# Spare row buffers joined, the four-head attention ended block by block, loads and readback moved in a four-layer graph network

## The chip, the cores and the metric

The kernel runs on one core of a Trainium2 chip. The number that counts is device time in microseconds (us), smaller is better; a profile shows one further execution of the same program, with every instruction on each engine: PE (TensorE matmuls; PEld its weight loads), DVE (VectorE), ACT (ScalarE), POOL (GpSimd) and SP (which only issues transfers). A name with a q, such as SPq or ACTq, is an engine's queue of issued work.

## What is computed

Four layers run over a graph of 2708 nodes with 256 features each. Every layer adds a graph attention over the neighbours and then a feed-forward part, both on layer-normed features. The change touches layer 1 (four attention heads, then a top-1 mixture of eight experts) and the beginnings of the attentions of layers 2 and 3. Cut to these:

```python
def L1_gnn(x, adj, W, a1, a2):                   # 4 heads of 64
    h = (x @ W).reshape(n, 4, 64)
    si = einsum('nhd,d->nh', h, a1); sj = einsum('nhd,d->nh', h, a2)
    e = leaky_relu(si[:, None, :] + sj[None, :, :], negative_slope=0.2)
    att = softmax(where(adj[:, :, None] > 0, e, -9e15), axis=1)
    return einsum('ijh,jhd->ihd', att, h).reshape(n, 256)

def L1_ffn(x, W1, b1, Wg, bg, Wd, bd):           # 8 experts
    H = gelu(x @ W1 + b1, approximate=False)     # 1024 wide
    probs = softmax(H @ Wg + bg)
    assign = argmax(probs)
    for e in range(8):
        out = out + where((assign == e)[:, None], probs[:, e:e+1] * (H @ Wd[e] + bd[e]), 0)
    return out

x = x + L1_gnn(layernorm(x), adj, ...)
x = x + L1_ffn(layernorm(x), ...)
x = x + L2_gnn(layernorm(x), adj, ...)           # one head, with a bias
x = x + L2_ffn(layernorm(x), ...)                # attention and a top-2 mixture
x = x + L3_gnn(layernorm(x), adj, ...)           # one head, then elu
x = x + L3_ffn(layernorm(x), ...)                # linear
```

## The kernel before

The nodes are 22 tiles of 128 rows (the last has 20), and most loops go by six blocks of 512 columns, that is four tiles each and two in the last. The residual X stays in the on-chip buffer for the whole program. The order of instructions on each engine is made by a scheduler from the program; `issue_after` holds one instruction behind another, and each engine takes its own list in that order.

`gat_heads` (L678) takes two heads in each of two passes p. For each source tile j it makes the masked weights e for the two heads on ACT (L674) and DVE (L675), and PE adds up the six accumulators of values (L780) and the denominators (L788) over all j. After the last j of a pass the denominators are copied (ds, L798), transposed, and inverted (rd, L803 and L806). Then each block's accumulator is copied out (o, L810), transposed (aux, L815), multiplied by the inverse (y, L822) and added to X (L829). Both passes end this way, and only then does `top1_ffn` begin.

`top1_ffn` (L857) has a front part by blocks. It loads the gate weights wg, biases and w1 on POOL's queue (L871 to L892) and the experts' weights wd, 8 MB, on SP's. The layer norm's sums and roots of all blocks are taken by `ln_stats`. For each block: `features` norms and transposes four tiles into ft, `hidden` makes 1024 hidden values per node (h, L911, then Gelu L915), `gate` makes the logits (pq L937, pr L943) and the routing bookkeeping, and `store` transposes the hidden values into rows (L926), copies them by DVE and ACT in turn into one of three buffers hr (L927), and writes them to a table in memory (`hidden`, L930, on SP's queue). The stores of the last two blocks come together at the end. The bookkeeping also scatters each node's number into a table by expert slot (fnodes, L1444).

Then come 26 expert steps of 128 slots each. The node numbers are read back from the table: the first eight steps by one load (L1554), whose every element of 4 bytes goes to its own partition, the others by one load each (L1550). They are cast to integers (L980) in groups of up to four steps, and POOL gathers the hidden rows by them (L990), five buffers deep and four steps ahead. Each step transposes its rows (ht, L1003, copied by DVE or ACT at L1004), multiplies by the expert's weights (y, L1035, two accumulators), adds the expert's bias bd (ys, L1041) and sends the rows to a table of results (L1573, POOL). During step 3 a `Head` (L1066) folds the score vectors of the next attention into its weight: loads g2w (L1074), av (L86) and g2bv (L1082), eight DVE operations at L657 and L660, and the bias's part (L1084 to L1089). Its loads and bd are issued on ACT's queue.

`gat_single` (L1092) is the attention of layers 2 and 3. It begins with `combine` (L1583): all results are read back (y, L1594), by SP's and ACT's queues in turn, and each block is weighted and added to X on DVE (L1604), followed by its statistics (L144, L145), the root on ACT (sd, L147), rstd (L151) and the normed tiles (L108) that PE transposes (tp, L1134). In layer 3 the mask of neighbours is also read back (`reload_graph`, L2088); `mark_empty` (L2080) writes two pieces of flags into it through ACT's queue. The same `mark_empty` runs before the four-head attention.

## Time and profile before

| | us |
|---|---|
| median of 3 runs (2875.14 to 2881.12) | 2879.4 |
| the profiled execution | 2876.56 |
| its span | 2874.8 |
| PE busy | 2630.7 |
| DVE busy | 1448.3 |
| ACT busy | 1037.4 |
| POOL busy | 369.4 |
| mean granted clock of PE, share of full speed | 0.951 |

The span is the time from the first to the last instruction of the profiled execution; 1.8 us lie around it. An engine's busy time leaves out the issuing of transfers and waiting on semaphores. The stages that the change touches lie at these places of the span: the four-head attention from 690 to 1068 us, the front part of the top-1 mixture from 1068 to 1209, the store and routing between 1209 and 1245, its expert steps from 1245 to 1360, the start of layer 2's attention from 1360 to 1374, and that of layer 3's from 2553 to 2578.

### The profile page before, as it was taken

The numbers are of one execution on the slowest core, as the hardware profiler recorded it, in microseconds if no ns is written. First come the engines' busy times: TensorE is split into PE (matmuls) and PEld (weight loads), VectorE is DVE, ScalarE is ACT, GpSimd is POOL, SyncE is SP. The second block draws the span as 40 slices with busy tenths as digits, with TensorE's granted clock in tenths as the row PEclk, the third lists the DMA queues.
The fourth block names the chain that finished last, engine by engine and source line by source line (L and its number), as shares of the span: only waits on it lengthen the run. The fifth ranks groups of instructions, "written<-read, shape, count | busy, mean of one in ns | idle before, by whom it ended". The sixth has DMA issues, their size and how long they took to land. (4 is left out here: it accounts for less than half of the span.)

```text
span 2874.8 us, 32363 instructions
## 1 busy us (share of the span) xinstructions
PE 2630.7 (92%) x11709; PEld 1604.0 (56%) x11709; DVE 1448.3 (50%) x3078; ACT 1037.4 (36%) x1636; POOL 369.4 (13%) x456
## 2 busy tenths in 40 slices
PE   5999989799999998979899899999969999969998
PEld 4667746563333334568688533333337777747885
DVE  7753358354777774432644456455653222235455
ACT  3344433224665653311543223233322222225453
POOL 0000012100000001133200023223331111110002
PEclk9999999698999998989999999899979999989999
DMA  8899210000000005253300100002031010041001
GB/s 296 290 301 327 81 65 1 8 1 1 1 1 1 1 17 176 82 173 108 114 1 0 34 22 17 15 0 93 15 116 32 30 34 30 30 147 49 1 1 39
DMA packets 113727, 197.67 MB, mean 69 GB/s; under 512 B 12380, under 2 KB 71636, under 8 KB 110732
## 3 DMA queue, kind: packets, MB, share of 16 engines
q1 hardware_dynamic: 92758, 147.89, 15.8%
q0 software_dynamic: 13120, 38.06, 4.1%
q10 hardware_dynamic: 7690, 9.62, 1.1%
q8 instruction: 98, 1.61, 0.2%
q14 instruction: 61, 0.50, 0.1%
HBM read 135.82 MB, written 59.71 MB: 68 GB/s over the span
## 5 line engine op out<-in xcount | busy, mean ns | idle before, releaser
L675 DVE SCALAR_TENSOR_TENSOR e<-e,mask 128x768 f32<-128x768 f32 (+2 forms) x264 | 411.5, 1573 | 311.0 <-ACT e L674 310.8
L674 ACT ACTIVATE e<-big_p,minus_one,ratio 128x768 f32<-128x768 f32 (+2 forms) x264 | 394.9, 1513 | 363.4 <-PE acc L1236 230.0
L1236 PE MATMUL acc<-V,e 128*128 128x257 f32 (+1 forms) x1936 | 433.5, 383 | 4.5 <-DVE e L675 4.4
L1236 PEld LDWEIGHTS acc<-V,e 128*128 128x128 f32 (+1 forms) x1936 | 352.4, 186 | 85.6 <-issue 32.1
L780 PE MATMUL acc<-e,V 128*64 128x512 f32 (+1 forms) x1056 | 249.7, 550 | 4.1 <-DVE e L675 4.1
L1909 PE MATMUL h<-w,ft 128*128 (+1 forms) x752 | 233.6, 453 | 0.5 <-ACT ft L1891 0.5
L284 PE MATMUL acc<-F,e 128*128 128x257 f32 x968 | 226.3, 384 | 2.9 <-DVE e L281 2.5
L284 PEld LDWEIGHTS acc<-F,e 128*128 128x128 f32 x968 | 173.5, 185 | 66.8 <-DVE e L281 28.1
L780 PEld LDWEIGHTS acc<-e,V 128*64 128x64 f32 x1056 | 95.4, 137 | 180.7 <-issue 159.1
L1736 PE MATMUL sc<-qt,kt 64*128 64x512 f32 (+5 forms) x568 | 176.6, 574 | 4.1 <-ACT e L1749 2.4
L1749 ACT ACTIVATE e<-sc 128x1024 f32<-128x1024 f32 (+3 forms) x120 | 99.6, 859 | 190.9 <-PE sc L1736 174.4
L1909 PEld LDWEIGHTS h<-w,ft 128*128 128x128 f32 x752 | 136.2, 191 | 56.7 <-issue 1.4
L281 DVE TENSOR_TENSOR e<-e,mask 128x512 f32<-128x512 f32 (+2 forms) x132 | 80.5, 625 | 150.4 <-ACT e L275 148.7
L1761 DVE TENSOR_TENSOR sum<-sum,e 128x1024 f32<-128x1024 f32 (+4 forms) x88 | 99.8, 1135 | 79.3 <-ACT e L1749 76.4
L275 ACT ACTIVATE e<-score 128x512 f32<-128x512 f32 (+2 forms) x132 | 69.7, 544 | 178.9 <-PE score L273 152.2
L1941 PE MATMUL po<-w,ht 114*128 (+1 forms) x564 | 129.5, 379 | 0.9 <-DVE ht L1934 0.9
L1755 PE MATMUL po<-e,V 128*64 128x512 f32 (+3 forms) x480 | 112.2, 549 | 16.8 <-ACT e L1749 8.7
L788 PE MATMUL den<-e,low 128*3 128x512 f32 (+1 forms) x1056 | 123.1, 542 | 0.0
L1941 PEld LDWEIGHTS po<-w,ht 114*128 114x128 f32 x564 | 106.7, 189 | 22.6 <-DVE ht L1934 8.2
L1563 DVE TENSOR_SCALAR second<-f,down 128x1 f32<-128x1 f32 x47 | 9.9, 212 | 213.0 <-DMA f<-hs 213.0
L273 PE MATMUL score<-QK 128*128 128x512 f32 (+2 forms) x264 | 112.1, 555 | 1.2 <-ACT e L275 0.7
L1736 PEld LDWEIGHTS sc<-qt,kt 64*128 64x128 f32 (+1 forms) x568 | 60.4, 189 | 92.5 <-issue 76.4
(606 smaller groups left out, 3496.3 us busy)
## 6 DMA issues: line engine op xcount, KB each, us to landing
row<-in_adj SPq DMA_DIRECT2D x21, 1354.0 KB
raw<-in_adjT SPq DMA_DIRECT2D x35, 768.0 KB
hs<-zero SPq DMA_DIRECT2D x8, 2838.0 KB
hidden<-hr SPq DMA_DIRECT2D x42, 256.0 KB
wd<-in_f_wd SPq DMA_DIRECT2D x8, 1024.0 KB
kept<-mask SPq DMA_DIRECT2D x21, 338.5 KB
mask<-kept SPq DMA_DIRECT2D x21, 338.5 KB
f<-hs SPq DMA_DIRECT2D x47, 129.0 KB
```

The costliest lines, as they stand in the source:

```text
L273: nc.tensor.matmul(ps[:r, :iw], QK[:, 0, span(j)], QK[:, 1, i0 : i0 + iw], start=True, stop=True)
L284: nc.tensor.matmul(acc[k][:ri], e[:r, k * P : k * P + ri], F[:r, j, :], start=j == 0, stop=j == NT - 1)
L674: nc.scalar.activation(v, big_p[:, i], AF.Relu, bias=net.minus_one, scale=ratio)
L675: return nc.vector.scalar_tensor_tensor(v, v, 1.0, net.mask[:, j, i], ALU.add, ALU.mult)
L780: nc.tensor.matmul(acc[n][half, :iw], V[:, j, h, :], e[:, k, i0 : i0 + iw], start=j == 0, stop=j == NT - 1)
L788: nc.tensor.matmul(den[g : g + Q, :iw], low[:, j, h, Q - 1 - q : 2 * Q - 1 - q], e[:, k, i0 : i0 + iw], start=False, stop=j == NT - 1 and ...
L1236: nc.tensor.matmul(acc[k][:ri], e[:, k * P : k * P + ri], V[:, j, :], start=j == 0, stop=j == NT - 1)
L1736: nc.tensor.matmul(by_pairs(ps[:r, g])[:, :, o:], kt[b, span(j)], qt[b, :, o:iw], start=True, stop=True)
L1755: nc.tensor.matmul(by_pairs(po[b])[:, :, o:], V[:r, j, g, :], by_pairs(e[:r, g])[:, :, o:], start=j == 0, stop=j == last,)
L1761: (nc.gpsimd if part else nc.vector).tensor_tensor(total, total, ev, ALU.add)
L1909: last = nc.tensor.matmul(halves[s, n][:, q, :HALF], fts[s][:, c, :], weights.w13[n][:, es[s], c, q * HALF : (q + 1) * HALF], start=c == 0 ...
L1941: last = nc.tensor.matmul(po, ht[:KP, k, :], w2[:KP, es[s], k, :], start=k == 0, stop=k == KC - 1)
```

## The change

- `gat_heads` is called inside `top1_ffn`. The copies o of all six blocks and the inverses rd are kept in a pool of their own. Pass 0 adds its blocks as before; pass 1 returns a function that adds one block. In the last step j of each pass the denominators come before the values; elsewhere after.
- `top1_ffn` adds block 0, takes its sums, adds block 1, and makes features of block 0; blocks 1 and 2 follow, then the hidden values of block 0; blocks 3 to 5 are added after that. `turn` chains these steps. The roots of blocks 1 to 5 are made on DVE by Newton steps (`newton`, some ten small operations per call), not on ACT.
- The experts' weights wd are placed where the kept copies were, and loaded two experts at a time after the stores of blocks 0 to 3.
- The stores of blocks 4 and 5 are all copied by ACT; the first eight of the twelve go through spare buffers: two of ft, cut in two, and one of the hidden halves, cut in four.
- The node numbers are read as rows of 128 (the first read as eight contiguous pieces of 512 bytes), transposed on PE and cast from there, in groups of eight and nine.
- bd is loaded on POOL's queue after the fourth gather; the head's three loads go to POOL's queue, after the send of step 3.
- In `gat_single` the zeroing of V and ratio goes from POOL to DVE, and a small root (`warm`) is asked of ACT at the start.
- `combine` reads by SP and POOL in turn, and by ACT only the second choice of block 0. The mask's reload is issued after the last read on POOL; the flags are written through POOL's queue.

```diff
-def gat_heads(net):
+def gat_heads(net, keep):
+    o = keep.tile([P, len(cols), 4 * P], F32, name="o")
+    rds = [keep.tile([P, 4, 4, Q], F32, name=f"rd{p}") for p in range(2)]
+    def add(p, n, psum, tag):
+        i0, iw = cols[n]
+        its = tiles_of(i0, iw)
+        pt = psum.tile([P, 4, P], F32, name="aux", tag=tag)
+        for c, i in enumerate(its):
+            r = rows(i)
+            nc.tensor.transpose(pt[:r, c, :], o[:, n, c * P : c * P + r], net.ident)
+        y = o[:, n, :].rearrange("p (c k d) -> p c k d", c=4, k=2)
+        for c0, c1, r in whole_and_rest(its):
+            d = rds[p].rearrange("p c (k b) q -> p c k b q", b=2)[:r, c0:c1, :, n // Q, n % Q]
+            nc.vector.tensor_tensor(
+                y[:r, c0:c1],
+                pt[:r, c0:c1, :].rearrange("p c (k d) -> p c k d", d=DH),
+                d.unsqueeze(3).to_broadcast([r, c1 - c0, 2, DH]),
+                ALU.mult,
+            )
+            xs = X[:r, its[0] + c0 : its[0] + c1, p * 2 * DH : (p + 1) * 2 * DH]
+            last = nc.vector.tensor_tensor(xs, xs, y[:r, c0:c1].rearrange("p c k d -> p c (k d)"), ALU.add)
+        return last
...
+            def values(e, j):
...
+            def weights(e, j):
...
+            for j in range(NT):
+                e = wide.tile([P, 2, N], F32, name="e")
+                for k, h in enumerate(heads):
+                    gat_pairs(net, e[:, k, :], j, 0, N, big_p[:, h, :], ratio[:, j, h : h + 1])
+                for step in (values, weights) if j + 1 < NT else (weights, values):
+                    with tc.issue_after(last.ins):
+                        last = step(e, j)
...
+                if p == 0:
+                    add(p, n, paux, "aux")
+    return lambda n, psum, tag: add(1, n, psum, tag)
...
+        held = ExitStack()
+        add = gat_heads(net, held.enter_context(tc.tile_pool(name="g1keep", bufs=1, side="right")))
-        wd = inner.enter_context(tc.tile_pool(name="f1wd", bufs=1, side="right")).tile([P, E, KC, D], F32, name="wd")
-        for e in range(E):
-            nc.sync.dma_start(wd[:, e], a["f1_wd"][e].rearrange("(c p) m -> p c m", p=P))
...
+            last = None
+            def turn(step, *args, **kw):
+                nonlocal last
+                with tc.issue_after(last.ins) if last else nullcontext():
+                    last = step(*args, **kw)
...
-            def store(its, halves):
+            def store(its, halves, late=False, room=()):
+                room = list(room)
                 for k, t in enumerate(its):
                     r = rows(t)
                     for n, half in enumerate(halves):
-                        hr = rp.tile([P, 512], F32, name="hr", bufs=3)
+                        hr = room.pop(0) if room else rp.tile([P, 512], F32, name="hr", bufs=3)
                         ps = pg.tile([P, 4, P], F32, name=f"hr{n}")
                         for c in range(KC // 2):
                             nc.tensor.transpose(ps[:r, c, :], half[:, c, k * P : k * P + r], net.ident)
-                        (nc.scalar.copy if n else nc.vector.tensor_copy)(
+                        (nc.scalar.copy if n or late else nc.vector.tensor_copy)(
                             hr[:r], ps[:r].rearrange("p c m -> p (c m)")
                         )
-                        nc.sync.dma_start(rows_of[span(t), n * 512 : (n + 1) * 512], hr[:r])
+                        last = nc.sync.dma_start(rows_of[span(t), n * 512 : (n + 1) * 512], hr[:r])
+                return last
...
+            tiles = [(tiles_of(*b)[0], tiles_of(*b)[-1] + 1) for b in blocks]
+            turn(add, 0, ptp, "tp")
+            turn(stats.sums, *tiles[0])
+            turn(add, 1, ptp, "tp")
+            turn(stats.roots, *tiles[0])
             ft = features(tiles_of(*blocks[0]))
+            turn(stats.sums, *tiles[1], root=False)
+            turn(add, 2, ptp, "tp")
+            turn(stats.sums, *tiles[2], root=False)
+            turn(stats.newton, rp, tiles[1][0], tiles[2][1])
             for n, (n0, nw) in enumerate(blocks):
                 its = tiles_of(n0, nw)
                 halves = hidden(ft, nw)
                 if n + 1 < len(blocks):
                     ft = features(tiles_of(*blocks[n + 1]))
+                if n == 0:
+                    for m in range(3, len(blocks)):
+                        turn(add, m, ptp, "tp")
+                        turn(stats.sums, *tiles[m], root=False)
+                    turn(stats.newton, rp, tiles[3][0], NT)
+                    last = None
+                    held.close()
+                    wd = inner.enter_context(tc.tile_pool(name="f1wd", bufs=1, side="right"))
+                    wd = wd.tile([P, E, KC, D], F32, name="wd")
                 gate(its, halves, nw)
                 kept.append((its, halves))
-                if n + 2 != len(blocks):
-                    for k in kept:
-                        store(*k)
-                    kept.clear()
+                if n + 2 < len(blocks):
+                    stored = store(*kept.pop())
+                    with tc.issue_after(stored.ins):
+                        for e in range(2 * n, 2 * n + 2):
+                            nc.sync.dma_start(wd[:, e], a["f1_wd"][e].rearrange("(c p) m -> p c m", p=P))
+            spare = [work.tile([P, 2, 512], F32, name="spare", tag="ft") for _ in range(2)]
+            spare.append(work.tile([P, KC // 2, 512], F32, name="spare", tag="ht512", bufs=3))
+            room = [t[:, k, :] for t in spare for k in range(t.shape[1])]
+            for k in kept:
+                store(*k, True, room)
+                room = ()
...
-            nc.scalar.dma_start(bd.rearrange("p e d -> p (e d)"), a["f1_bd"].rearrange("e d -> (e d)").partition_broadcast(P))
...
+            groups = [range(E)] + [range(s, min(s + 9, usual)) for s in range(E, usual, 9)]
+            rowed = sp.tile([P, P], F32, name="rowed", bufs=1)
             held = {}
-            def numbers(group):
+            def load(group, at):
+                node = rowed[at : at + len(group), :]
+                if group[0] == 0:
+                    route.load_first(node)
+                else:
+                    for k, s in enumerate(group):
+                        route.load(s, node[k : k + 1, :])
+            def numbers(group, at):
                 g = slice(group[0], group[-1] + 1)
-                nc.vector.tensor_copy(number[:, g], node[:, g])
-            def places(group):
+                here = slice(at, at + len(group))
+                ps = pt.tile([P, len(group)], F32, name="node", bufs=1)
+                nc.tensor.transpose(ps, rowed[here, :], net.ident[here, here])
+                nc.vector.tensor_copy(number[:, g], ps)
+                return ps
...
+            for n, g in enumerate(groups):
+                load(g, 32 * n)
+            first = numbers(groups[0], 0)
             for s in range(4):
-                fetch(s)
+                fetched = fetch(s)
+            with tc.issue_after(fetched.ins):
+                nc.gpsimd.dma_start(
+                    bd.rearrange("p e d -> p (e d)"), a["f1_bd"].rearrange("e d -> (e d)").partition_broadcast(P)
+                )
...
-                    route.send(to[:, s : s + 1], y)
-                    with tc.issue_after(added.ins):
-                        for g in groups[1:]:
+                    sent = route.send(to[:, s : s + 1], y)
+                    with tc.issue_after(added.ins), tc.issue_after(sent.ins):
+                        for n, g in enumerate(groups):
                             if s + 6 == g[0]:
-                                numbers(g)
-                                places(g)
+                                places(g, numbers(g, 32 * n))
                         if s == 3:
-                            heads.append(Head(net, prep, one, "g2", True, nc.scalar))
+                            heads.append(Head(net, prep, one, "g2", True))
...
-        nc.gpsimd.memset(V[:, LAST], 0.0)
-        nc.gpsimd.memset(ratio[:, LAST:], 0.0)
+        nc.vector.memset(V[:, LAST], 0.0)
+        nc.vector.memset(ratio[:, LAST:], 0.0)
+        nc.scalar.activation(small.tile([P, 1], F32, name="warm", bufs=1), net.ln_eps, AF.Sqrt)
...
-        self.loaded = sync.dma_start(f, self.hs[bass.ds(row, P), :])
+        rows_of = self.hs[bass.ds(row, P), :]
+        self.loaded = sync.dma_start(f, rows_of.rearrange("p d -> d p") if self.choices == 1 else rows_of)
     def load_first(self, f):
         self.loaded = self.net.nc.sync.dma_start(
-            f, self.hs.rearrange("(e c) d -> c (e d)", e=self.E)[:P, :]
+            f, self.hs.rearrange("(e c) d -> e (c d)", e=self.E)[:, :P]
...
+        queues = nc.sync, nc.gpsimd
...
-                    (nc.sync, nc.scalar)[(n + c) % 2].dma_start(
+                    engine = nc.scalar if n == 0 and c else queues[(n + c) % 2]
+                    read = engine.dma_start(
                         y[:r, k0:k1, :],
                         self.ys[r0 : r0 + (k1 - k0 - 1) * P + r, :].rearrange("(t p) d -> p t d", p=r),
                     )
+                    if engine is nc.gpsimd:
+                        self.read = read
...
-        reload_graph(net, kept)
+        with net.tc.issue_after(route.read.ins):
+            reload_graph(net, kept)
...
-        gat_heads(net)
...
-    net.nc.scalar.dma_start(row[:, :whole], net.flags[:LAST])
-    net.nc.scalar.dma_start(row[:, whole:], net.flags[LAST:NT, : N - whole])
+    net.nc.gpsimd.dma_start(row[:, :whole], net.flags[:LAST])
+    net.nc.gpsimd.dma_start(row[:, whole:], net.flags[LAST:NT, : N - whole])
```

The order of the pools in `gat_heads` also changes; `Stats` (L126) and `inverse_root` (L307) are as before.

## The prediction

> **What bounds the kernel now.** I read the engine totals first, then the forty slices and the chain of waits, then windows and timelines of the places that the edits touch.
>
> ```profile
> PE 2630.7 (92%) x11709; PEld 1604.0 (56%) x11709; DVE 1448.3 (50%) x3078; ACT 1037.4 (36%) x1636; POOL 369.4 (13%) x456
> ```
>
> TensorE works in 92% of the 2874.8 us span, so 244 us are idle, and they lie in the seams between stages. The chain of waits is followed back only to about 2146 us, so the earlier seams had to be read by windows. The columns below are window, length, busy time (and instructions) of PE, PEld, DVE, ACT, POOL, granted clock, DMA share, GB/s.
>
> ```profile
> 1068.23:1093.36 25.13, 9.50 (x37) 5.44 (x36) 23.34 (x92) 3.65 (x8) 4.63 (x13) 0.56 0.60 185
> 1093.36:1110.16 16.80, 16.80 (x36) 7.47 (x37) 2.41 (x7) 6.09 (x8) 0.00 (x0) 0.85 0.92 293
> 1110.16:1131.50 21.34, 21.31 (x96) 11.26 (x95) 7.21 (x28) 7.73 (x12) 4.00 (x4) 1.00 0.27 100
> ```
>
> Seam A is the first line: from the last denominator matmul of the four-head attention to the first hidden matmul (h, L911). VectorE is the busy one, 23.3 of 25.1 us: it adds all six blocks and takes their statistics before block 0 may go. Lines two and three are hidden(0) and the rest of the first block; there PE is full and DVE has room.
>
> Seam B is the end of that front part. Timeline columns: start, length, engine, line, operation, and in brackets the idle time before it and its releaser.
>
> ```profile
> 1223.27 0.58 ACT L927 COPY hr<-hr 128x512 f32<-128x512 f32 x1 [7.29 <-DMA hidden<-hr]
> 1226.53 0.68 DVE L927 COPY hr<-hr 20x512 f32<-20x512 f32 x1 [0.69 <-DMA hidden<-hr]
> 1231.44 0.41 SPq L1554 DMA_DIRECT2D node<-fnodes  x1
> 1238.78 0.17 DVE L980 CAST number<-node 128x8 int32<-128x8 f32 x1 [6.26 <-DMA node<-fnodes]
> 1239.84 1.00 POOL L990 DMA_INDIRECT hr<-hidden,number  x1 [22.18 <-DMA node<-fnodes]
> 1245.11 1.30 PE L1003 MATMUL ht<-ident,hr 128*128 128x128 f32 x5 [17.14 <-issue]
> ```
>
> Row copies wait for stores to free three buffers; the table read starts when all stores are in, takes 7.3 us to the cast, and the gather another 5.3 us. In the expert steps after it nothing waits long, and the fold of the next layer's scores runs at once:
>
> ```profile
> 1265.55 0.42 DVE L1041 TENSOR_TENSOR ys<-y,bd 128x256 f32<-128x256 f32 x1 [2.73 <-PE y L1035]
> 1265.89 0.41 DVE L657 TENSOR_TENSOR a1t<-g2w,av 128x256 f32<-128x256 f32 x1
> 1270.79 0.68 DVE L1004 COPY ht<-ht 128x512 f32<-128x512 f32 x1
> ```
>
> Seam D, from the decoder's experts to the last attention:
>
> ```profile
> 2557.22 12.66 ACTq L1594 DMA_DIRECT2D y<-dys  x7
> 2562.37 3.26 DVE L1604 SCALAR_TENSOR_TENSOR X<-y,dweight,X 128x256 f32<-128x256 f32 x8 [6.58 <-DMA y<-dys]
> 2575.12 1.28 ACT L147 ACT_TABLE_LOAD   x1 [22.31 <-DMA y<-dys]
> 2576.74 0.18 DVE L151 RECIPROCAL rstd<-sd 128x4 f32<-128x4 f32 x1 [6.23 <-ACT sd L147]
> 2577.52 1.73 PE L1134 MATMUL tp<-ident,f 128*128 128x128 f32 x7 [25.12 <-DVE f L108]
> ```
>
> The statistics of block 0 were ready at 2567.4, yet ACT takes the root only at 2576.4, because its queue is still issuing and waiting for loads.
>
> **Seam A, block-by-block end: -10.** The last step's matmuls are the same, in another order; the denominator's copy (0.69) and transposes now pass under the values. I count from the end of the last matmul, 1068.23. Removed ahead of h: the adds and statistics of blocks 3 to 5, and waits between. What stays in DVE's order: the copy of add (1.09), the copy of o (0.99 with its tail), rd and reciprocal (0.65), two blocks of y and X (4 x 0.69 = 2.7), block 0's statistics (1.9), then for four tiles normed (0.38), PE transposes, copy (0.39), with the waits seen now in the last two tiles, about 4. That sums to 11.3; I take 11.5. The loads of w1 are issued where they were, 3.8 us after the last matmul, and landed 5.2 later, at 9.0: just covered; if they took hyout's 12.7 us instead, h would start at 16.5. So h moves from 25.1 to 11.5: -13.6. Given back: the last three blocks' ten transposes (1.11 + 1.08 + 0.69 us at half clock, some 1.6 warm) now stand in a full PE. DVE's work for these blocks, 3.2 + 3.2 + 1.9, and ten small operations of the inverse root (2), is 10.3 us; added to 7.2 busy of 21.3 in that block it is 17.5, so throughput covers it. But DVE obeys order: the gate's copies and the row copies stand behind, PE waits for them, and ten of those 10 us are the upper price. I take 2. Net -10, bounds -13.6 and -2.
>
> **Block loads of the expert weights: 0.** Eight megabytes leave the stretch 1081 to 1112 and go in four parts behind the stores of blocks 0 to 3 on SP. Each part of 2 MB at the 348 GB/s of that stretch is 6 us; a block lasts 21, and the next stores come in its second half. Without that cover the row copies would wait up to 6 us per block, against ACT and DVE that are a third busy.
>
> **Spare row buffers: -6.** Twelve copies at 0.58 on ACT alone, with transposes, need about 9 us from 1209.7, where now the last is at 1228.5. The transfers cannot be drained so fast: the DMA share from 1210 to 1229 (0.71, 0.75, 0.86, 0.49 over 4 us each, 0.31 over 3) makes 12.2 us of full engines, so the end of all stores lies between 1222 and the present 1231. The twelfth copy also still waits for the ninth store. I take 1225.4, -6; bounds -9 and 0.
>
> **Table order: -3.4.** The first read has 8 descriptors rather than 1024 elements. Small loads landed in 2.1 to 3.0 us, the gathers in 5.2; I take 3.0. To it come a transpose (0.43, cold) and two hand-overs, 0.9 together. 7.3 - 3.0 - 0.9 = 3.4; bounds -4.3 and -1.2. Transposes and casts of the later groups cost PE under 1 us, in steps of 4.33 us.
>
> **Later bias loads: +3.4.** The bias bd is asked for after the fourth gather and first needed 7.5 us after PE starts; w1, as large and on the same queue, landed in 5.2, so it is covered. The head's three loads are worse. They go to POOL behind the send of step 3, which issued at 1266.25 (0.99); g2w follows at 1267.55. The g3 head did exactly this:
>
> ```profile
> 2149.07 0.79 POOL L1074 DMA_DIRECT2D g3w<-in_g_w  x1 [0.30 <-issue]
> 2155.04 0.43 DVE L657 TENSOR_TENSOR a1t<-g3w,av 128x256 f32<-128x256 f32 x1 [2.84 <-DMA av<-in_g_a]
> ```
>
> 5.9 us from issue to first use, so the fold starts at 1273.5, where now it starts at 1265.89. It waits in DVE's queue with ys of step 4 and the copy ht of step 6 behind it. Eight fold operations 0.33 apart (2.7), bt 0.6, ys 0.33, grow 0.6, ht 0.69 end at 1278.4; PE needs ht of step 6 at about 1275 (ys of step 5 was at 1274.21, plus transposes). The stall is 3.4; bounds 0 (loads in 2.1) and 6.
>
> The Trainium skill prices it lower: "DMA: Bandwidth & Descriptors", in its anatomy of a GpSimd-issued transfer, fits about 2.0 us plus bytes over 436e3 per us, 2.6 us for 256 KB. By that the fold would start near 1271 and the stall be about 1 us, the total 2.4 lower. The rows (3.8 and 5.1 us to landing) differ from it.
>
> **Readback, seam C: 0.** X waits for the first load on SP, which stays. The second block's load goes from ACT to POOL; it may land 1 us later, but DVE reaches it 3.3 us after the first. The root's table load (1365.77) was already over before it was needed, so asking for it early changes nothing here. The memsets of V and ratio (0.31, 0.10) pass from POOL to DVE, which idles until 1368.21. Bounds -1 and +1.
>
> **Readback, seam D: -5.** ACT keeps one load, so the root follows the statistics at 2567.4. Next late is DVE itself: the combination of block 1 stands ahead of rstd and ends at 2570.5; rstd and normed bring PE to 2571.3 rather than 2577.5, -6.2. Three queues at once instead of two may delay block 0's pair: a third 0.5 MB at 349 GB/s is 1.5 us. I take -5; bounds -6.2 and 0. The mask reload starts about as before and is needed 35 us later.
>
> A rule speaks against this: the same page ("SWDGE vs HWDGE vs iDMA") wants plain transfers on SP or ACT, not GpSimd. By it alone the term would be 0 or a loss; the row shows ACT's issuing as the thing waited for, so I keep the gain.
>
> **Start of the attention: -0.6.** The two flag loads (0.88, 0.75) leave ACT ahead of the first e; part of that was waiting on PE anyway. Bounds -1 and 0.
>
> **Sum.** -10 + 0 - 6 - 3.4 + 3.4 + 0 - 5 - 0.6 = -21.6. The profiled execution took 2876.6, so 2855.0. The median of the runs stood 2.8 above that execution; I add half and forecast 2856. A 0.2% difference, 5.8 us, is about what can be told from no change.
>
> **Rivals.** (1) The stores of seam B end when they do now, because the transfers and not the buffers are the limit: for it, a DMA share of 0.86 at only 65 GB/s around 1220; against it, the drop to 0.31 at the end. Time 2862. (2) The pushed-back DVE work of seam A lies wholly on PE's path: for it, in-order waits; against it, 14 idle DVE us in the block. Time 2856 + 8 = 2864. (3) Slower: TensorE's clock stays at 0.5 through hidden(0) and the next block, because h now comes in pieces between transposes waiting for DVE. For it, 0.56 in seam A; against it, the clock was 0.94 four us after h had begun. 16.8 us at 0.85 become 28.6, 21.3 become 42.6: +33, time 2889; it decides once the lost clock exceeds 22 us. (4) All bounds favourable: below 2844.
>
> **Chances.** Forecast 2846 to 2860: 0.50; rival 1 0.16; rival 2 0.15; rival 3 0.10; rival 4 0.06; a mix that ends within 0.2% 0.03. Range 2844 to 2872 from the terms' bounds. Faster 0.86, same 0.03, slower 0.11.
>
> **What would show it.** First h about 11 to 12 us after the last values matmul; 12 stores without buffer waits until the last; the cast 4 us after the table read; a DVE wait of 6 to 8 us for av in front of the fold, with one gap of PE of 3 us; sd of the last attention right after its statistics. I am wrong if PE shows gaps in the first two blocks, or if the loads through POOL arrive later than X asks for them.

## The result

| | before | after |
|---|---|---|
| median of 4 runs, us | 2879.62 (2875.14 to 2881.12) | 2850.05 (2846.85 to 2853.26) |
| profiled execution / its span, us | 2876.56 / 2874.8 | 2853.26 / 2851.6 |
| mean granted clock | 0.951 | 0.955 |

The ratio is 0.990 with a 95% interval of 0.988 to 0.992: 1.0% faster. The forecast was 2856 in a range of 2844 to 2872. The two spans differ by 23.2 us. Cut at the same events in both traces, they differ here:

| stretch, from event to event | before | after | difference | predicted |
|---|---|---|---|---|
| start to the first values matmul | 697.12 | 697.04 | -0.1 | -0.6 |
| four-head attention, both passes, to its last matmul | 371.11 | 366.97 | -4.1 | 0 |
| seam A: to the first h | 25.13 | 11.05 | -14.1 | -13.6 |
| front part: first h to the last gate matmul (pq) | 115.10 | 120.21 | +5.1 | +3.6 |
| seam B: last pq to the table's first read | 22.98 | 20.72 | -2.3 | -6 |
| seam B: read to cast | 7.34 | 1.93 | -5.4 | -3.4 |
| seam B: cast to the first expert transpose | 6.33 | 5.30 | -1.0 | 0 |
| expert steps, to the last ys | 114.80 | 119.46 | +4.7 | +3.4 |
| seam C: last ys to the first tp of layer 2 | 14.03 | 13.38 | -0.6 | 0 |
| layer 2, to the last send of the decoder's experts | 1179.14 | 1180.42 | +1.3 | 0 |
| seam D: last send to the first tp of layer 3 | 24.44 | 17.64 | -6.8 | -5 |
| the rest | 297.28 | 297.48 | +0.2 | 0 |

The engine totals of the page after the change: PE's busy time is 5.4 us shorter than it was, though it has three more matmuls; the other 17.8 of the 23.2 are idle time that is gone.

```profile
PE 2625.3 (92%) x11712; PEld 1616.6 (57%) x11712; DVE 1446.4 (51%) x3086; ACT 1040.0 (36%) x1639; POOL 381.5 (13%) x470
```

Seam A and the first two blocks in windows of the kernel after (window, length, busy time and instructions of PE, PEld, DVE, ACT, POOL, granted clock, DMA share, GB/s):

```profile
1064.01:1075.06 11.05, 4.76 (x25) 3.37 (x25) 10.05 (x40) 2.02 (x3) 4.49 (x13) 0.70 0.37 107
1075.06:1091.20 16.14, 15.78 (x34) 6.62 (x34) 7.00 (x30) 5.98 (x8) 0.00 (x0) 0.89 0.00 0
1091.20:1114.00 22.80, 22.80 (x110) 12.56 (x109) 16.52 (x75) 7.71 (x12) 2.34 (x3) 1.00 0.37 125
1114.00:1135.00 21.00, 18.42 (x91) 9.94 (x90) 9.37 (x34) 5.81 (x10) 4.58 (x5) 1.00 0.55 166
```

DVE is still the busy one in the seam (10.05 of 11.05), with less than half of its earlier work. What was pushed back is in the third line: 16.5 us of DVE beside a full PE. The clock in the first h stretch is 0.89, so rival 3, a clock that stays at 0.5, found no ground. The fourth line is new: PE is idle for 2.6 us in the second block. The timeline there (start, length, engine, line, operation, and in brackets the idle time before it with its releaser):

```profile
1126.69 0.69 DVE L961 COPY hr<-hr 128x512 f32<-128x512 f32 x1 [3.52 <-DMA hidden<-hr]
1127.52 1.07 PE L960 MATMUL hr<-ident,ht 128*128 128x128 f32 x8 [2.52 <-DVE flogits L979]
```

DVE's row copy waits 3.5 us for a store to free its buffer; the logits (flogits, L979) stand behind it in DVE's order, and PE behind those. The prediction had named gaps of PE in the first two blocks as a sign of being wrong. This is such a gap; the section on the experts' weights below traces it to loads, not to the pushed-back work that the sign was meant for.

Seam B in the kernel after:

```profile
1213.60 0.57 ACT L961 COPY hr<-hr 20x512 f32<-20x512 f32 x1 [4.90 <-DMA hidden<-hr]
1215.99 0.28 SPq L1629 DMA_DIRECT2D rowed<-fnodes  x1
1217.92 0.17 DVE L1050 CAST number<-node 128x8 int32<-128x8 f32 x1 [0.27 <-PE node L1049]
1218.89 1.00 POOL L1061 DMA_INDIRECT hr<-hidden,number  x1 [14.72 <-DMA rowed<-fnodes]
1223.22 3.98 PE L1074 MATMUL ht<-ident,hr 128*128 128x128 f32 x16 [5.34 <-DMA hr<-hidden,number]
```

The last copy still waits 4.9 us for a store, and the read still starts 2.4 us after that copy began. But the read in the new order is transposed and cast 1.93 us after its issue.

The head of layer 2's attention in the expert steps:

```profile
1246.55 0.78 POOL L1146 DMA_DIRECT2D g2w<-in_g_w  x1
1252.32 0.42 DVE L657 TENSOR_TENSOR a1t<-g2w,av 128x256 f32<-128x256 f32 x1 [6.29 <-DMA av<-in_g_a]
1257.24 3.72 PE L1110 MATMUL y<-wd,ht 128*128 128x256 f32 x16 [2.91 <-DVE g2grow L1161]
```

DVE idles 6.3 us for av, and PE 2.9 us behind the last of the fold's operations.

Seam D. The last send is at 2536.48:

```profile
2540.03 0.46 ACTq L1673 DMA_DIRECT2D y<-dys  x1
2540.52 4.17 POOL L1673 DMA_DIRECT2D y<-dys  x6 [3.07 <-DMA dys<-y,to]
2545.29 3.26 DVE L1685 SCALAR_TENSOR_TENSOR X<-y,dweight,X 128x256 f32<-128x256 f32 x8 [7.72 <-DMA y<-dys]
2550.22 3.23 DVE L1685 SCALAR_TENSOR_TENSOR X<-y,dweight,X 128x256 f32<-128x256 f32 x8
2550.34 0.30 ACT L147 ACTIVATE sd<-mv,ln_eps 128x4 f32<-128x4 f32 x1 [11.70 <-DVE mv L145]
2553.36 0.17 DVE L151 RECIPROCAL rstd<-sd 128x4 f32<-128x4 f32 x1
2554.12 1.73 PE L1208 MATMUL tp<-ident,f 128*128 128x128 f32 x7 [18.32 <-DVE f L108]
```

The root sd comes 5.05 us after block 0's combination began (14.04 before), released by the statistics and no longer by a load. Next late is DVE's own order: rstd stands behind the combination of block 1, as the prediction had it. From the start of block 0's combination to the first transpose it took 15.15 us before and 8.83 after, -6.3. The other 0.5 of the seam's 6.8 is an earlier arrival of block 0's results (8.81 us after the last send, 9.29 before), and that scatters: 8.0 to 10.0 us in the kernels below.

### The profile page after: what moved, and what is told of

The parts are those of the page before. It is cut to its first block, busy times and chain, and to the rows that moved or that the text cites. A ratio compares the mean times of both kernels' runs of the same rounds, so it can differ in the third digit from the quotient of the medians.

```text
span 2851.6 us, 32365 instructions
## 1 busy us (share of the span) xinstructions
PE 2625.3 (92%) x11712; PEld 1616.6 (57%) x11712; DVE 1446.4 (51%) x3086; ACT 1040.0 (36%) x1639; POOL 381.5 (13%) x470
## 4 chain that ended last, share of the span: by engine, by line
PE 74%; DVE 9%; issue 5%; DMA 5%; ACT 3%; POOL 3%; another core or an unknown queue 0%; ACTq 0%; SPq 0%; POOLq 0%; DVEq 0%
PE acc L1310 15%; PE acc L805 8%; PE acc L284 7%; PE den L816 4%; PE po L2022 4%; PE po L1836 3%; PE sc L1817 3%; PE score L273 3%; PE pv L123 3%; PE h L1990 3%; DMA f<-hs 2%; PE h L943 2%; PE po L123 2%; PE sc L1785 2%; PE pl L123 1%
## 5 line engine op out<-in xcount | busy, mean ns | idle before, releaser
L675 DVE SCALAR_TENSOR_TENSOR e<-e,mask 128x768 f32<-128x768 f32 (+2 forms) x264 | 411.3, 1573 | 310.2 <-ACT e L674 309.9
L805 PEld LDWEIGHTS acc<-e,V 128*64 128x64 f32 x1056 | 107.5, 137 | 163.8 <-issue 131.2
L1836 PE MATMUL po<-e,V 128*64 128x512 f32 (+3 forms) x480 | 111.7, 547 | 16.8 <-ACT e L1830 8.7
```

What stands on the lines that cost most here:

```text
L675: return nc.vector.scalar_tensor_tensor(v, v, 1.0, net.mask[:, j, i], ALU.add, ALU.mult)
L805: made = nc.tensor.matmul(acc[n][half, :iw], V[:, j, h, :], e[:, k, i0 : i0 + iw], start=j == 0, stop=j == NT - 1)
L1836: nc.tensor.matmul(by_pairs(po[b])[:, :, o:], V[:r, j, g, :], by_pairs(e[:r, g])[:, :, o:], start=j == 0, stop=j == last,)
```

## The experiments

Twelve kernels were run, each a small edit of the changed kernel, and each but the last was timed once. Single times scatter too much to read one or two us from: layer 2, whose code no edit touches, lasted 1170.2 to 1186.1 us in the profiles. So each experiment is judged by the stretches of the table above that its edit touches, against the same stretch in the kernels that left that part alone. These scatter as follows: passes 365.4 to 367.0; seam A 11.04 to 11.11; front part 119.6 to 123.0; last pq to read 20.4 to 21.6; expert steps 118.3 to 122.3 (mean of eleven 120.3); seam D 17.1 to 18.3; the rest 296.6 to 297.5.

### The unforeseen gain in the attention

Step by step, all of it lies at the start of pass 1. The denominators of its third step begin 35.0 us after the pass's first instruction before, 30.3 us after the change; from then on two steps take 16.1 us in both. In the timelines of VectorE there, before and then after, the lines of L675 are the masking that each step's matmuls need:

```profile
882.99 2.97 DVE L675 SCALAR_TENSOR_TENSOR e<-e,mask 128x2708 f32<-128x2708 f32 x1
900.78 2.97 DVE L675 SCALAR_TENSOR_TENSOR e<-e,mask 128x2708 f32<-128x2708 f32 x1
904.47 8.79 DVE L675 SCALAR_TENSOR_TENSOR e<-e,mask 128x2708 f32<-128x2708 f32 x3
```

```profile
884.56 2.97 DVE L675 SCALAR_TENSOR_TENSOR e<-e,mask 128x2708 f32<-128x2708 f32 x1
893.57 2.97 DVE L675 SCALAR_TENSOR_TENSOR e<-e,mask 128x2708 f32<-128x2708 f32 x1
897.66 2.97 DVE L675 SCALAR_TENSOR_TENSOR e<-e,mask 128x2708 f32<-128x2708 f32 x1
```

Before, DVE masks nothing between 886 and 900.8, and the third step's 24 values matmuls then took 7.66 us where 24 take 5.2 to 5.7 in that pass's steady steps. After, the masking comes between the pieces of the end of pass 0. The timelines of ACT, before and then after, show what the masking waited for:

```profile
892.71 0.59 ACT L810 COPY o<-acc 128x512 f32<-128x512 f32 x1 [10.23 <-PE aux L815]
898.00 5.18 ACT L674 ACTIVATE e<-big_p,minus_one,ratio 128x2708 f32<-128x2708 f32 x2 [4.71 <-PE acc L780]
```

```profile
890.53 5.19 ACT L674 ACTIVATE e<-big_p,minus_one,ratio 128x2708 f32<-128x2708 f32 x2 [7.58 <-PE den L816]
```

ACT makes the next e 20.9 us after the pass's first instruction before, 13.1 after. Before, ACT's last copy of an accumulator waited 10.2 us for earlier copies to be transposed, and e then 4.7 us more for PE's values. PE counts as busy in both: a matmul that is fed late shows as a longer one. Two parts of the change bear on this: six places for the accumulators' copies instead of three, and the forced order of values and denominators.

**Three places again** (`e2_three_slots`):

```diff
+    def slot(p, n):
+        return n if p else n % 3
-            nc.tensor.transpose(pt[:r, c, :], o[:, n, c * P : c * P + r], net.ident)
+            nc.tensor.transpose(pt[:r, c, :], o[:, slot(p, n), c * P : c * P + r], net.ident)
...
-                (nc.vector.tensor_copy if n % 2 else nc.scalar.copy)(o[:, n, :iw], acc[n][:, :iw])
+                (nc.vector.tensor_copy if n % 2 else nc.scalar.copy)(o[:, slot(p, n), :iw], acc[n][:, :iw])
```

> The changed kernel, but in the first pass of the four-head attention the six copies of the accumulators share three places, as they shared three buffers before. The second pass took 191.1 us before (877.15 to 1068.23) and 186.6 us after (877.45 to 1064.01), which the prediction did not foresee. Theory: with three places the second half of the accumulators stays occupied until the first adds are done, so the second pass's first matmuls wait; then the second pass lasts about 190 to 191 us again. Rival: the fixed order of values and denominators makes it; then it stays at 186.6 us.

Pass 1 took 189.85 us against 186.58, +3.3, with a plain wait in the timeline of PE:

```profile
881.78 0.66 PE L704 MATMUL aux<-ident,o 128*128 128x128 f32 x4 [0.51 <-DVE o L709]
885.87 0.66 PE L704 MATMUL aux<-ident,o 128*128 128x128 f32 x4 [3.44 <-DVE o L709]
```

Both passes took 368.7 us, 1.7 to 3.3 more than with six places, and 2.4 less than before. ACT's copy waits for a place again, and the next e comes 21.4 us after the pass's first instruction, as late as before (timeline of ACT):

```profile
887.10 0.59 ACT L849 COPY o<-acc 128x512 f32<-128x512 f32 x1 [6.60 <-DVE X L716]
896.61 5.18 ACT L674 ACTIVATE e<-big_p,minus_one,ratio 128x2708 f32<-128x2708 f32 x2 [8.92 <-PE den L819]
```

So the six places carry a good part of the gain. The 2.4 us that three places do not give back are not explained.

**The order left to the scheduler** (`e3_free_order`):

```diff
-                for step in (values, weights) if j + 1 < NT else (weights, values):
-                    with tc.issue_after(last.ins):
-                        last = step(e, j)
+                values(e, j)
+                weights(e, j)
```

> The forced order of values and denominators in the four-head attention is taken out: the scheduler places them, values first. Theory: the last step with its denominators ahead of the values is what lets the denominator's copy and transposes pass under matmuls, so from the last values matmul's end to the first hidden matmul 11.05 grows by 1 to 2.5 us, and pass 1 (186.6 us) shrinks by as much as its order cost, or stays within 0.5. Rival: the order also carries the 1.2 us of pass 1 that the six places for copies do not explain; then pass 1 grows by about 1.2.

From the last attention matmul to h it took 11.98 us instead of 11.05, below the expected range. The passes together took 365.0, 0.4 below the shortest unchanged ones, and from the first values matmul to h 376.98 against 376.4 to 378.0. The border between the passes moved with the order, so pass 1 alone (181.3) says nothing. So the order wins 0.9 us in the seam, but over the passes and the seam together it is worth nothing that can be seen, and the rival falls too.

### The head's loads in the expert steps

**On ACT's queue, as before the change** (`e1_head_act`):

```diff
-                            heads.append(Head(net, prep, one, "g2", True))
+                            heads.append(Head(net, prep, one, "g2", True, nc.scalar))
```

> The changed kernel with one edit undone: the head's three loads are on ACT's queue again. Theory: the late loads cost the expert steps one TensorE gap of 2.9 us, because the fold waits in VectorE's order (6.3 us for av in the changed kernel's profile) with ys and ht behind it; then the wait for av is gone, no gap of 2.9 us, the stretch from the first ht transpose to the last ys falls from 119.5 us to about 116.5, and the span from 2851.6 to about 2848.7. Rival: the fold's own 5 us of VectorE work make the gap, whenever it runs; then a gap of about 3 us stays and the stretch stays at 119.

The expert steps took 116.73 us, 2.7 less than in the changed kernel and 1.6 below the shortest of the eleven that left them alone. The fold follows ys at once; the idle time in brackets is gone, and so is PE's gap:

```profile
1250.23 0.43 DVE L1116 TENSOR_TENSOR ys<-y,bd 128x256 f32<-128x256 f32 x1 [3.07 <-PE y L1110]
1250.57 0.41 DVE L657 TENSOR_TENSOR a1t<-g2w,av 128x256 f32<-128x256 f32 x1
```

So the move of these loads to POOL costs about 3 us, as forecast. The remaining 1.9 of the +4.7 stands in `e13_best_fine` too, which has the same edit (116.64); what makes it is open. The whole span did not fall to the 2848.7 expected: it was 2854.3, with a front part 2.4 us longer and a start 2.3 longer, neither of which the edit touches.

### The stores of the hidden rows

**No spare places** (`e4_no_spare`) and **spare places for all twelve copies** (`e5_all_spare`):

```diff
-                store(*k, True, room)
+                store(*k, True)
```

```diff
+            more = work.tile([P, 2, HID], F32, name="spare", tag="w1", bufs=1)
+            room += [more[:, k, h * 512 : (h + 1) * 512] for k in range(2) for h in range(2)]
             for k in kept:
                 store(*k, True, room)
-                room = ()
+                room = room[8:]
```

> The changed kernel with the twelve last stores through the three row buffers again (all copies still on ACT). The stretch from the last gate matmul to the table read was 23.0 us before, 20.7 to 21.1 in the changed kernel, 19.3 with four more places. Theory (buffers set it): about 23 us. Rival (only the transfers and ACT's copies set it): within 1 us of 21.

> The changed kernel with four more spare places, cut from the first layer's weights w1, so that each of the twelve last stores has its own. In the changed kernel the last copy waited 4.9 us for a store, and the table read began 20.7 us after the last gate matmul. Theory (buffers): without that wait the table read begins 3 to 5 us sooner. Rival (transfers): the stores themselves take that long; the last copy is earlier, but the table read begins within 1 us of where it did.

Last pq to read: 22.48 us without, 20.4 to 21.6 with eight, 19.26 with twelve. Against the mean of the kernels with eight (20.9), eight places are worth about 1.6 us, and the other four as much again: less than the theory of `e5_all_spare` and more than its rival. With twelve no copy waits for a store, and yet the read comes late (timeline and one window of this kernel):

```profile
1208.26 0.57 ACT L961 COPY spare<-hr 20x512 f32<-20x512 f32 x1 [0.28 <-PE hr L960]
1214.65 0.32 SPq L1631 DMA_DIRECT2D rowed<-fnodes  x1
```

```profile
1208.00:1212.00 4.00, 0.23 (x2) 0.00 (x0) 0.00 (x0) 0.57 (x1) 0.00 (x0) 0.50 1.02 125
```

The last copy is done 13.4 us after the last pq, where it was 18.9 with eight places, the last store is issued by 1209.2, and the transfers run on at a share of 1.02 until 1212 (the packets' times added up, over the time of 16 engines). The read waits for the stores themselves to land. So with twelve places the transfers are the bound: the mechanism of rival 1 of the prediction, after 3.2 us that buffers could win.

### The loads of the experts' weights

Four kernels moved the 8 MB of wd among the stores.

**Later, in three parts** (`e6_wd_later`):

```diff
-                        for e in range(2 * n, 2 * n + 2):
+                        for e in ((), range(0, 3), range(3, 6), range(6, 8))[n]:
```

> The changed kernel, with the experts' weights loaded three, three and two at a time after the stores of blocks 1, 2 and 3, none after block 0. In the changed kernel TensorE is idle 2.6 us in the second block (18.4 busy of 21.0 from 1114 to 1135), behind a row copy that waited 3.5 us for a store. Theory: the 2 MB loaded ahead of that block's stores delay them; then the gap in the second block goes and the front part is about 2.5 us shorter, unless the same gap comes up in the third block. Rival: the gap comes from VectorE's pushed-back work and the shared row buffers; then it stays.

The gap in the second block was gone, but two larger ones came in the blocks whose stores now met 3 MB of loads (timeline of PE), and the front part took 127.85 us, +7.6:

```profile
1151.83 1.94 PE L960 MATMUL hr<-ident,ht 128*128 128x128 f32 x8 [5.29 <-DVE flogits L979]
1178.96 1.94 PE L960 MATMUL hr<-ident,ht 128*128 128x128 f32 x8 [3.19 <-DVE flogits L979]
```

The changed kernel and the eight others that load 2 MB after block 0 all have the gap in the second block, 2.5 to 3.8 us long, with the same releaser. So the loads make it, and the pushed-back work, which is the same here, does not.

**On ACT's queue** (`e10_wd_act`) and **in pieces of 0.5 MB behind each tile's stores** (`e11_wd_fine`):

```diff
-                            nc.sync.dma_start(wd[:, e], a["f1_wd"][e].rearrange("(c p) m -> p c m", p=P))
+                            nc.scalar.dma_start(wd[:, e], a["f1_wd"][e].rearrange("(c p) m -> p c m", p=P))
```

```diff
+                    for e, c in parts[k : k + 1]:
+                        w4 = a["f1_wd"][e].rearrange("(c p) m -> p c m", p=P)[:, c : c + 4]
+                        with tc.issue_after(last.ins):
+                            last = nc.sync.dma_start(wd[:, e, c : c + 4], w4)
```

> The changed kernel with the eight loads of the experts' weights on ACT's queue in place of SP's, so that no store of hidden rows stands behind them in a queue. After the runs so far the front part (first h to the last gate matmul) lasts 120.2 to 122.6 us, against 115.1 before, and 127.9 where three parts of the weights stand ahead of a block's stores. Theory: the stores wait behind the weights in SP's queue; then the front part falls by 2 to 5 us, to about 118. Rival: it is the shared transfer engines, whatever the queue; then it stays at 120 to 122, or the gap moves.

> The changed kernel with the weights loaded in pieces of 0.5 MB, one after each tile's two stores, on SP's queue. Theory (weights ahead of stores delay them, by their size): a piece delays the next stores by 1.5 us at 350 GB/s, less than the 1 to 3 us between stores, so the front part falls to about 118 us. Rival: total traffic in the blocks decides, not its grain; then 120 to 122 us.

On ACT's queue the front part took 128.48 us, +8.3. SP's queue then held stores alone, and still ACT's row copies waited for them (timeline of ACT):

```profile
1112.64 0.58 ACT L961 COPY hr<-hr 128x512 f32<-128x512 f32 x1 [7.55 <-DMA hidden<-hr]
1155.76 0.58 ACT L961 COPY hr<-hr 128x512 f32<-128x512 f32 x1 [7.48 <-DMA hidden<-hr]
```

So another queue does not part loads from stores. The Trainium skill says so under "Issuing engines are not separate DMA queues" in "DMA: Bandwidth & Descriptors": transfers started by different engines run on the same transfer engines. The run agrees. The 8.3 us are not the price of that alone: the eight loads also went out closer together, from 1103.9 to 1145.4 us instead of 1110.0 to 1179.9, and PE's gaps are now mostly waits for ACT, which issues them. In small pieces the front part took 120.00, nothing that can be told from the scatter; the rival holds, though the gap is down to 1.5 us (2.3 in `e13_best_fine`). What the loads cost in the changed kernel as it stands was not isolated: the gap in block two is 2.5 us, the front part is 5.1 longer, 2.1 of that is more time of PE at work, and its scatter is 3. A kernel without these loads was not tried.

### The last seam

**Readback on SP and ACT in turn, as before the change** (`e7_read_act`):

```diff
-                    engine = nc.scalar if n == 0 and c else queues[(n + c) % 2]
+                    engine = (nc.sync, nc.scalar)[(n + c) % 2]
...
-        with net.tc.issue_after(route.read.ins):
-            reload_graph(net, kept)
+        reload_graph(net, kept)
```

> The changed kernel with the results read back through SP's and ACT's queues in turn, as before, and the mask's reload not held behind them; the early root on ACT and the zeroing on VectorE stay. Before, the last send of the decoder lay 24.4 us ahead of the first transpose of the last attention; in the changed kernel 17.6. Theory: ACT's queue, full of loads, held up the root; then about 24 us. Rival: the early root, which brings the table load forward by itself, made the difference; then about 18 to 19. The layer 2 seam (14.0 before, 13.4 after) should stay within 1 us in both.

Seam D took 19.47 us, +1.8 of the 6.8; from the start of the combination to the first transpose it was 10.80, +2.0 of the 6.3. ACT's loads hold the root, which is now released by a load again:

```profile
2539.49 14.79 ACTq L1673 DMA_DIRECT2D y<-dys  x7
2554.33 0.30 ACT L147 ACTIVATE sd<-mv,ln_eps 128x4 f32<-128x4 f32 x1 [16.04 <-DMA y<-dys]
2554.66 0.18 DVE L151 RECIPROCAL rstd<-sd 128x4 f32<-128x4 f32 x1 [1.89 <-ACT sd L147]
```

The root comes 9.70 us after block 0's combination began, 4.65 later than after the change. Only 1.9 of that reaches rstd, because DVE is at block 1 until then. So the theory, 24 us, falls short: ACT's readback alone is not the cause. Three things could make up the rest: the early root that loads ACT's table, the flags' loads taken off ACT, and the order behind them.

**No early root** (`e8_no_warm`):

```diff
-        nc.scalar.activation(small.tile([P, 1], F32, name="warm", bufs=1), net.ln_eps, AF.Sqrt)
```

> The early root of each attention is taken away (it computes a value that nothing reads); the readback on SP and POOL and the later mask reload stay. Theory: with ACT's queue free of loads, the root's table load comes where the statistics of block 0 ask for it, and VectorE reaches rstd 3 us later anyway: seam D (17.6 us after the last send) grows by 0 to 1.3 us, one table load. Rival: the early request is what pulls the table load out of the stall, and seam D goes back towards 20 us or more (+2.5 to +6).

Seam D took 18.21 us, inside the scatter, and the root stood 5.04 us after the combination's start, as with the early root. The timeline of ACT shows why:

```profile
2536.39 1.28 ACT L147 ACT_TABLE_LOAD   x1 [4.81 <-DMA dys<-y,to]
2546.28 0.30 ACT L147 ACTIVATE sd<-mv,ln_eps 128x4 f32<-128x4 f32 x1 [8.61 <-DVE mv L145]
```

The table load does not need asking for here: with one load on ACT's queue it runs 8.6 us ahead of the root by itself. The seam is as the theory had it, but not for its reason, since the table load does not wait for the statistics. With the rest of the change in place, this line of it is worth nothing.

**Flags back on ACT** (`e14_flags_act`):

```diff
-    net.nc.gpsimd.dma_start(row[:, :whole], net.flags[:LAST])
-    net.nc.gpsimd.dma_start(row[:, whole:], net.flags[LAST:NT, : N - whole])
+    net.nc.scalar.dma_start(row[:, :whole], net.flags[:LAST])
+    net.nc.scalar.dma_start(row[:, whole:], net.flags[LAST:NT, : N - whole])
```

> The two loads of the mask's flags go back from GpSimd to ACT, all else stays: in the last seam they stand in ACT's queue, held until the first readback is in and the mask's memory may be written. Theory: an ACT queue that waits to issue a load is what made the inverse root late, so the root of block 0 comes behind the flags and seam D (17.6) grows by 3 us or more. Rival: the hold ends before the statistics are ready, and seam D stays within 0.7 us of 17.6; then the move of the flags was worth nothing there. Start to the first values matmul: +0.1 at most.

```profile
2546.13 0.30 ACT L147 ACTIVATE sd<-mv,ln_eps 128x4 f32<-128x4 f32 x1 [12.90 <-DVE mv L145]
2546.59 1.28 ACTq L2165 DMA_DIRECT2D mask<-flags  x1
2552.47 0.76 ACTq L2166 DMA_DIRECT2D mask<-flags  x1
2553.28 0.38 ACT L1214 ACTIVATE ft<-tp 128x256 f32<-128x256 f32 x1 [6.86 <-DMA y<-dys]
```

The theory falls for the root: held behind the readback, the flags come after it, and sd stands at its 5.04 us. Seam D took 18.78, of which 1.1 is a later landing of the first readback (9.95 us after the last send instead of 8.81); from there to the first transpose it is 8.83 as ever. But the flags then hold ACT until 2553.2 with the first ft behind them, and the rest of the kernel took 299.28 us, +1.8. Before, ACT's stretch of issuing loads ended 16.8 us after the last send, the flags 22.0, the table load 23.3, all ahead of the root. Each of the three was put back singly, and none of them alone brings back more than 2.0 of the 6.3. That they together held the root, one behind the other, is read from the trace before; no kernel with two or three of them put back was run.

### The three edits together

`e13_best_fine` is e1, e5 and e11 in one kernel.

> Three edits together: the loads of the next layer's head on ACT's queue, four more spare places for the last row copies, and the expert weights in pieces of 0.5 MB behind each tile's stores. If they add up: the experts' stretch 119.5 becomes 116.8, the end of seam B's copies 20.7 becomes 19.0, the stretch from the first hidden to the last gate matmul stays at 120 to 121.5; the median is 4 us below the changed kernel's 2850, 2846, and the ratio to the kernel before 0.988. Rival: what one stretch gains the layer after it gives back by the granted clock, whose swings (about 10 us in unchanged code) are larger than the edits: 2850 and 0.990.

The median of four runs is 2849.2 us (2842.25 to 2855.16), the ratio to the kernel before 0.989 with an interval of 0.986 to 0.991. That cannot be told from the changed kernel's 0.990. The expert steps gained as alone (116.64), the front part is at 119.99, but last pq to read took 22.94 us, 3.7 more than e5's. The timeline of ACT:

```profile
1214.72 0.38 ACTq L1149 DMA_DIRECT2D g2w<-in_g_w  x1
1215.14 0.57 ACT L961 COPY spare<-hr 20x512 f32<-20x512 f32 x1 [6.63 <-DMA hidden<-spare]
```

The head's first load stands ahead of the last two row copies in ACT's order. By the trace its wait of 6.6 us ends when a store of hidden rows lands, and it is issued only at 1214.72; the copies, which in `e5_all_spare` waited for PE alone, stand behind it. The two gains undo each other by the order of one queue. The clock rival named the right total, but this is not its mechanism.

## Why the prediction held, and where not

The forecast is 6 us above the median, inside the range. Of that, 1.7 us are the terms, 1.0 is what was added for the median (the half of 2.8 that it names would be 1.4), and 3.2 that the profiled execution after lies above its own median. The terms' errors are larger than their sum, so that the total came so near is in part luck.

- **Seam A** is right in mechanism and size: -14.1 for -13.6. This is read from the two traces (DVE's work ahead of h fell from 23.34 to 10.05 us); of its edits only the forced order was undone in a run. Of the 3.6 to be given back, 2.1 us shows as more time of PE at work in the front part; its three pushed-back blocks cost no wait in the block where they run (22.80 of 22.80). Rivals 2 and 3 had no ground.
- **The attention's passes** were counted as "the same, in another order". That is the step with the largest omission, 4.1 us: it considered the end of pass 1 and not the same code at the end of pass 0, where copies that wait for a place hold up ACT's next e, and with it DVE's masking and PE.
- **Block loads of wd, 0:** the working named the price ("row copies would wait up to 6 us per block") and then called it covered, since the next stores come in a block's second half and ACT and DVE are a third busy. But PE waits for DVE's logits, which stand behind a waiting copy. One gap of 2.5 us remained, and 3 MB in a block made 3.2 to 5.3. It is the sign that the prediction named for itself, with another cause.
- **Spare buffers, -6:** mis-sized; about -1.6 (e4). The prediction took a point between draining the transfers and the present end; e5 shows that even without any buffer wait only 3.2 us are to be had, since from there on the transfers set the end.
- **Table order, -3.4:** the mechanism is right, the read was faster: 1.65 us from issue to the transpose, where 3.0 had been taken from small loads elsewhere. The saving is 5.4.
- **Later bias loads, +3.4:** right; DVE idles 6.3 us, PE 2.9, and e1 takes it back. The trace has 5.8 us from g2w's issue to the fold, and the row of the other head (5.97 us, which the working rounds to 5.9) was the better guide. An estimate by the fit in the Trainium skill ("DMA: Bandwidth & Descriptors", the section "Anatomy of one DMA", which gives it for one transfer) had made the stall about 1 us; here three loads stand in a row.
- **Readback, seam D, -5:** -6.8 in one pair of profiles; by the mean of the ten kernels that left seam D alone (17.7) it is -6.7. The part from block 0's combination on is -6.3, the -6.2 that the working had found before it allowed 1.5 for a third queue; no run shows that delay (8.81 us after the send, 9.29 before). What the prediction called ACT's issuing was more than one thing: the readback, worth 2.0 us when it alone is put back, then the flags and the table load that stood behind it.
- **Seam C and the start:** the start moved by less than it scatters, seam C by about as much.

By the table, terms that brought less than forecast make 8.5 us (the spare places 3.7 of it) and those that brought more make 10.0 (the passes 4.1, the table and gather 3.0, seam D 1.8), so they nearly cancel, by luck. Part of each is scatter.

## What to carry to other kernels

A buffer wait in front of a store says which instruction is late, not what makes it late: add buffers only after reading the transfer share behind it. When a stage's end is put in pieces, look at every place where that code runs, above all where the engine that ends one pass also feeds the next. An engine that computes and also issues loads takes both in one order: in these runs a load that had to wait on ACT, whether a readback, a flag or a weight for later, held the computation behind it, for 2 to 7 us. Ask what stands behind a load before asking which queue is the fastest.

## What was not expected of the chip

The same instructions of layer 2 took 1170 to 1186 us in different profiles, and in a pair of them the granted clock shows where. Here are the same 25 us of layer 2, 475 us after its first tp, in the kernel after and in e8, whose code is the same there:

```profile
1831.06:1856.06 25.00, 24.73 (x78) 8.14 (x77) 9.09 (x8) 7.77 (x9) 2.35 (x1) 0.76 0.00 0
```

```profile
1833.11:1858.11 25.00, 24.10 (x91) 8.52 (x89) 11.29 (x11) 8.71 (x10) 3.63 (x2) 1.00 0.00 0
```

PE is busy nearly all the time in both; at a clock of 0.76 it finished 78 matmuls and at 1.00 it finished 91. Layer 2 was 1180.4 us long in the first and 1173.8 in the second. At the faster pace its 78 matmuls would have taken some 3.6 us less, an estimate from these two lines. This one stretch is worth as much as the larger edits above, so a kernel's total says little about an edit of 2 us, and `e11_wd_fine`'s 2843.79, the lowest time of the kernels that ran once, comes with a layer 2 of 1170.2. What sets the granted clock there is not shown.

Two row copies of the changed kernel at 1202.6 and 1205.5 waited 2.5 and 2.3 us for a releaser that the trace names only as "remote". What that is stays open.
